# Step 0 of a sparse attention kernel in 105 steps a tile: TensorE's products laid on other steps, with more steps between VectorE and TensorE

## The chip, the cores and the metric

The kernel runs on one core of a Trainium2 chip. The core has five engines that run side by side, each through its own queue of instructions in order: TensorE (PE, matrix products, with a queue of weight loads, PEld), VectorE (DVE), ScalarE (ACT), GpSimd (POOL) and SyncE (SP, which here only issues DMAs). An instruction that needs the result of another engine waits at the head of its queue, and all that stands behind it waits too. The metric is the device time of one execution in microseconds (us), as the median of several runs.

## The reference

Two layers work on 3327 nodes with 256 features. Layer 0 is a graph attention over a sparse 0/1 adjacency with a gated update. Layer 1 makes two steps of a propagation over that adjacency and, beside it, of an attention that keeps for each row only the largest probabilities up to a sum of 0.9:

```python
def _top_p_attention(X, W1, W2, W3):
    q = X @ W1.T @ W2.T
    k = X @ W3.T
    logits = q @ k.T / TAU
    probs = jax.nn.softmax(logits, axis=-1)
    idx = jnp.argsort(-probs, axis=-1)
    sp = jnp.take_along_axis(probs, idx, axis=-1)
    cs = jnp.cumsum(sp, axis=-1)
    keep_sorted = cs - sp < TOP_P
    ...
    A = probs * mask
    return A / jnp.maximum(A.sum(-1, keepdims=True), 1e-12)
...
for n in range(STEPS):                 # STEPS = 2
    A = _top_p_attention(Xa, W1, W2, W3)
    Xf = R @ Xf
    Xa = A @ Xa
    Z = Z + Xf @ U1[n].T + Xa @ U2[n].T
```

Each layer ends with a layer norm over the input plus the layer's result. The change is in the first of the two steps (n = 0, "step 0").

## The kernel before

The 3327 rows are 26 tiles of 128 (the last has 127). Layer 0 runs to about 400 us, step 0 of layer 1 from there to about 1000 us, then step 1, then the layer's end. In step 0 few keys are kept by a whole tile of 128 rows, so the kernel does not multiply by all 3327 keys: it finds the keys that any row of the tile keeps (at most 640), gathers those, and works the attention out on them alone. For one tile (function `sparse`), in this order, with the names that the profile uses:

- pl: logits of the tile against all keys, in four pairs of products of 416 columns (L1542), copied by ACT to SBUF (`array`, L1545). DVE takes the eight largest of each group of 208 (the "eights", L1558) and sorts these candidates into a list of 40 (L1576, L1578); nmax is minus the largest.
- g1, m1, pxf: POOL gathers the neighbours' rows of x (L631), DVE makes a 0/1 matrix (m, L1286), PE multiplies (pxf, L1299 and L1301), ACT scales (xf, L1317), and a DMA writes the rows out. This is R @ Xf. xb (L1715) is a sum that POOL makes for the end of the layer.
- Exp of all logits with their sums (L1306, L1312) and of the list (e, L1314); a running sum and comparisons (L1322 to L1340) give `limit`, for each row minus a threshold between the lowest logit kept and the highest dropped.
- Signs of logits minus limit (ACT L1345, L1347; DVE L1350, is_ge) are summed over the rows by 26 small products (pc, L1355); any (L1362) says which keys some row keeps, two products (pp) number them, and DVE works out from that two one-hot matrices (upto L1370 to high L1382; hot L1387, L1389, L1390, L1392). Their 26 products (pu, L1397) are the list of kept keys. It goes over node (ACT L1402, DVE L1404) through DRAM and back (L1405, L1407).
- POOL turns it into row numbers (uidx, L1410) and gathers the kept keys' rows (g from x1k, five gathers, L1414). PE transposes the keys (pk, L1435 and L1437), ACT copies them (kg), PE makes the logits of the kept keys minus limit (plt, L1448 and L1454; diag holds limit), ACT takes Exp (w, L1460), DVE sets those under the limit to 0 (w, L1462), PE multiplies with the rows (pav, L1466), DVE takes the reciprocal of the sum (rA, L1469), ACT scales (xa, L1473), and `qk` makes query and key of step 1 (ptq, xtq, pq, qT, kT).

`sparse` is a generator. `yield from to(n)` lets n - done phases go by, so that a tile's work is cut into steps. `step_0` (L1480) starts a tile every EVERY0 = 16 phases and in each phase runs every tile that is under way one step further, the oldest first. About six tiles are in work at any time, and what runs together is what has the same step number modulo 16. The order so written is the order of the queues of PE, ACT, DVE and POOL (`manual_schedule`). Waits between engines are put in by the framework, by regions of tiles that overlap. `first_1` fetches the rows for step 1's first tile and, as tiles end, makes its logits; the last pair of these needs all 26 tiles. Tiles of psum and SBUF come from pools with a fixed number of buffers (`bufs`), and taking one waits until the use before last (with two) has been read. The pool `psm` with its tag "sm" has two and serves pc, pp, pu, ptq and pq.

The call of each tile at its phase:

```python
while self.phase < EVERY0 * NT or tiles:
    if self.phase % EVERY0 == 0 and self.phase // EVERY0 < NT:
        tiles.append(self.sparse(self.phase // EVERY0))
    for g in list(tiles):
        if next(g, True):
            tiles.remove(g)
            self.done += 1
```

## Time and profile before

| what | us |
|---|---|
| median of 3 runs | 1859.94 (1857.53 to 1861.38) |
| the profiled execution | 1862.22, its span 1860.4 |
| busy in the span: PE, DVE, POOL, ACT | 1565.4, 1442.2, 1083.6, 1032.6 |
| DVE's first instruction of step 0's list (upto), tile 0 and tile 25 | 418.5 and 952.7 |
| PE busy, 600 to 700 us, at a granted clock of 0.86 | 83.44 of 100 |
| DVE busy, 600 to 700 us | 79.94 of 100 |
| PE busy, 1100 to 1400 us (step 1), clock 1.00 | 290.21 of 300 |

The page counts an engine as busy while an instruction runs; a wait is put down to the instruction that ended last before it. Lines "A <- B: us, times, longest" name the instruction that waited and the one waited for. In the timeline a row has the start, the duration, the engine, the line in the kernel, the operation with output and inputs, the count of equal instructions put together, and in brackets the idle time before it. "Granted clock" is the share of full speed that PE had.

### The profile page before, as it was taken

Reading aid. Unit: us, or ns where it says so; the run is one execution under the profiler, and the core shown is the slowest. Engines: PE = TensorE matmul, PEld = TensorE weight load, DVE = VectorE, ACT = ScalarE, POOL = GpSimd, SP = SyncE. Lnnn points to the kernel's source line nnn. Section 1 sums busy time; section 2 is a strip of 40 time slices with the busy share of each in tenths; the row PEclk is TensorE's granted clock in tenths of the full one; section 3 lists DMA queues with packets and bytes.
Section 4 is the critical chain, followed back from the end, with each engine's and each line's share of the span. In section 5 each row is a group of like instructions: output and inputs, shape, how many; then the busy total and the mean of one; then the engine's idle time right before and its main releaser. Section 6 shows DMA issues by size and latency. Waiting matters only on the chain. (4 is left out here: it accounts for less than half of the span.)

```text
span 1860.4 us, 28927 instructions
## 1 busy us (share of the span) xinstructions
PE 1565.4 (84%) x8425; PEld 1105.7 (59%) x8425; DVE 1442.2 (78%) x4835; ACT 1032.6 (56%) x2388; POOL 1083.6 (58%) x1800
## 2 busy tenths in 40 slices
PE   6489998986788888788876999999999989788992
PEld 5255555644555555555544777777777656677882
DVE  5788887358887888888736999999999877967751
ACT  3366666645655666565633555555555536568554
POOL 2577777535555555555463666556666573756654
PEclk9799999977888888888877999999999989899996
DMA  8877773232333333333331111111111120223321
GB/s 272 298 255 231 232 229 86 69 88 76 90 91 84 85 82 94 91 89 91 93 81 36 46 49 46 46 49 53 53 50 52 47 59 21 69 60 99 98 88 45
DMA packets 113862, 180.07 MB, mean 97 GB/s; under 512 B 27740, under 2 KB 82773, under 8 KB 113696
## 3 DMA queue, kind: packets, MB, share of 16 engines
q0 software_dynamic: 26624, 74.64, 15.2%
q1 hardware_dynamic: 68818, 86.65, 14.4%
q10 hardware_dynamic: 18254, 16.86, 2.8%
q8 instruction: 69, 1.13, 0.3%
q14 instruction: 97, 0.79, 0.1%
HBM read 146.08 MB, written 32.09 MB: 96 GB/s over the span
## 5 line engine op out<-in xcount | busy, mean ns | idle before, releaser
L1759 PE MATMUL pav<-xa,at 128*128 128x256 f32 (+2 forms) x1352 | 329.6, 388 | 7.3 <-ACT at L1745 7.0
L1545 ACT COPY array<-pl 128x416 f32<-128x416 f32 (+3 forms) x402 | 183.2, 508 | 209.2 <-PE pl L1542 201.8
L1759 PEld LDWEIGHTS pav<-xa,at 128*128 128x128 f32 (+2 forms) x1352 | 244.8, 190 | 86.6 <-ACT at L1745 39.2
L1558 DVE MAX8 cand<-array 128x8 f32<-128x167 f32 (+5 forms) x921 | 244.0, 337 | 18.6 <-ACT array L1545 15.0
L1542 PE MATMUL pl<-kT,qT 64*128 64x416 f32 (+3 forms) x804 | 224.2, 588 | 16.9 <-ACT array L1545 11.4
L631 POOL DMA_INDIRECT g<-xf_rows,edge x130 | 136.7, 1052 | 154.8 <-PE pxf L1702 124.2
L1745 ACT COPY at<-pt 128x512 f32<-128x512 f32 (+2 forms) x182 | 96.1, 542 | 138.0 <-PE pt L1743 87.2
L631 POOL DMA_INDIRECT g<-whx,edge x130 | 140.9, 1084 | 46.7 <-issue 36.0
L631 POOL DMA_INDIRECT g<-x_rows,edge x130 | 137.1, 1054 | 50.9 <-issue 43.9
L1414 POOL DMA_INDIRECT g<-x1k,uidx x130 | 140.8, 1083 | 39.0 <-issue 31.7
L1466 PE MATMUL pav<-g,w 128*128 128x257 f32 (+1 forms) x260 | 106.8, 588 | 31.9 <-DVE w L1462 29.5
L1576 DVE MAX8 lst<-cand 128x8 f32<-128x160 f32 (+3 forms) x364 | 114.1, 313 | 8.1
L1542 PEld LDWEIGHTS pl<-kT,qT 64*128 64x128 f32 (+1 forms) x804 | 77.7, 195 | 65.1 <-issue 29.4
L1466 PEld LDWEIGHTS pav<-g,w 128*128 128x128 f32 (+1 forms) x260 | 76.7, 307 | 54.0 <-DVE w L1462 32.1
L848 DVE FIND_INDEX8 at<-ones,array 128x8 uint32<-128x840 f32 (+1 forms) x104 | 105.5, 1027 | 0.0
L1371 POOL COPY needed<-upto 128x1 f32<-128x1 f32 x26 | 4.8, 185 | 158.5 <-DVE upto L1370 158.5
L1674 DVE MATCH_REPLACE8 array<-gone,array 128x3335 f32<-128x3335 f32 (+1 forms) x26 | 94.0, 3617 | 0.0
L1578 DVE MATCH_REPLACE8 cand<-lst,cand 128x160 f32<-128x160 f32 (+3 forms) x312 | 92.9, 298 | 0.0
L1694 POOL TENSOR_SCALAR m<-col,erow 128x128 f32<-128x128 f32 x130 | 76.8, 604 | 1.0
L1301 PE MATMUL pxf<-g,m 128*128 128x256 f32 (+1 forms) x260 | 69.4, 416 | 1.9 <-DMA g<-x_rows,edge 1.2
L969 PE MATMUL acc<-g,m 128*128 128x259 f32 (+1 forms) x260 | 64.9, 397 | 6.8 <-ACT m L965 6.8
L1702 PEld LDWEIGHTS pxf<-g,m 128*128 128x128 f32 (+1 forms) x260 | 49.4, 198 | 34.0 <-issue 24.0
(564 smaller groups left out, 3869.7 us busy)
## 6 DMA issues: line engine op xcount, KB each, us to landing
array<-in_adj_dram SPq DMA_DIRECT2D x23, 1248.0 KB
array<-in_adj_dram SPq DMA_DIRECT2D x23, 415.5 KB
xf_rows<-xf SPq DMA_DIRECT2D x50, 128.0 KB
xa_rows<-xa SPq DMA_DIRECT2D x50, 128.0 KB
xfs<-xf_rows SPq DMA_DIRECT2D x50, 128.0 KB
whx<-table ACTq DMA_DIRECT2D x25, 129.5 KB
x_rows<-x ACTq DMA_DIRECT2D x25, 128.0 KB
x1k<-x ACTq DMA_DIRECT2D x25, 128.0 KB
```

What stands on the lines that cost most here:

```text
L631: self.nc.gpsimd.indirect_dma_start(out=dst[:, b, :], out_offset=None, in_=table[:, :], in_offset=bass.IndirectOffsetOnAxis(ap=self.edge[: ...
L848: nc.vector.max_index(at[:r, g, :], self.ones8[:r], ad[:r, g, :])
L1414: nc.gpsimd.indirect_dma_start(out=g2[:, b, :], out_offset=None, in_=sh.x1k[:, :], in_offset=bass.IndirectOffsetOnAxis(ap=idx[:, b : b + 1 ...
L1466: nc.tensor.matmul(acc[:r, : D + 1], w[:, b, :r], g2[:, b, : D + 1], start=(b == 0), stop=(b == UB - 1))
L1542: nc.tensor.matmul(pl[:r, :w], q[on], self.sh.kT[on, n, s : s + w], start=True, stop=True)
L1545: nc.scalar.copy(l[:r, h * HALF + s : h * HALF + s + w], pl[:r, :w])
L1558: self.nc.vector.max(cand[:r, g * 8 : g * 8 + 8], src[:r, g * group : min(N, (g + 1) * group)])
L1576: nc.vector.max(lst[:r, k : k + 8], cand[:r])
L1578: nc.vector.match_replace(cand[:r], lst[:r, k : k + 8], cand[:r], -BIG)
L1674: nc.vector.match_replace(rev, gone[:r], rev, -BIG)
L1745: nc.scalar.copy(at[:, :full, :r], pt[:, :full, :r])
L1759: nc.tensor.matmul(v.acc[: v.r, :D], at[:k, j - 4 * g, : v.r], V[:k, j, :], start=(j == 0), stop=(j == NT - 1))
```

## The change

The same work is laid on other steps. A tile takes 105 steps in place of 93; EVERY0 stays 16, so that between six and seven tiles are in work at a time. In a table (place = step modulo 16):

| work | engine | step before (place) | step after (place) |
|---|---|---|---|
| m1 | DVE | 15 (15) | 7 (7) |
| pxf, six pairs of products | PE | 18 (2) | 21 and 22 (5, 6) |
| xf and its rows out | ACT, SP | 23 (7) | 25 (9) |
| bound, is_ge | DVE | 29 (13) | 30 (14) |
| pc | PE | 33 (1) | 33 (1) |
| any | DVE | 35 (3) | 36 (4) |
| pp | PE | 36 (4) | 38 (6) |
| upto to high | DVE | 37 (5) | 43 (11) |
| hot, four products | DVE | 38, 39, 39, 43 (6, 7, 7, 11) | 45, 47, 47, 53 (13, 15, 15, 5) |
| pu | PE | 45 (13) | 57 (9) |
| node copy; node sum, list out and back | ACT; DVE, SP | 47; 49 (15; 1) | 59; 61 (11; 13) |
| uidx and five gathers | POOL | 56 to 61 (8 to 13) | 69 to 74 (5 to 10) |
| diag; pk | ACT; PE | 67 (3) | 75; 77 (11; 13) |
| kg; plt; w's Exp | ACT; PE; ACT | 70; 72; 74 (6; 8; 10) | 79; 82; 84 (15; 2; 4) |
| w's mask; pav; rA | DVE; PE; DVE | 78; 80; 83 (14; 0; 3) | 86; 89; 93 (6; 9; 13) |
| xa and its rows out | ACT, SP | 87 (7) | 95 (15) |
| ptq; xtq; pq; qT and kT | PE; ACT; PE; ACT | 89; 89; 91; 91 (9, 11) | 98; 100; 102; 104 (2, 4, 6, 8) |

The copy of the number of kept keys (needed) goes from POOL to DVE. `first_1` starts at phase 431 in place of 430. The logits, eights, sort, Exps and the gathers of g1 keep their steps. The diff:

```diff
--- before.py
+++ after.py
@@ -1280,7 +1280,7 @@
                 sh.gather(g1, sh.x1_rows, t, ((1, 2, 3, 5, 6).index(step),))
             if step == 7:
                 self.x_and_bias(t)
-            if step == 15:
+            if step == 7:
                 m1 = work.tile([P, EB, P], F32, tag="m", name=f"m{tag}")
                 for b in range(EB):
                     nc.vector.tensor_scalar(m1[:, b, :], sh.col1, sh.erow[:, t, b : b + 1], None, ALU.is_equal)
@@ -1295,10 +1295,6 @@
         yield from to(18)
         next(sort)
         next(sort)
-        acc1 = self.pac.tile([P, 512], F32, tag="av", name=f"pxf{tag}")
-        nc.tensor.matmul(acc1[:r, :D], self.ident[:r, :r], sh.x1[:r, t, :], start=True, stop=False)
-        for b in range(EB):
-            nc.tensor.matmul(acc1[:r, :D], m1[:, b, :r], g1[:, b, :], start=False, stop=(b == EB - 1))
         both = self.p[t % 2].bitcast(BF16)
         signs, hot = both[:, : N + 1], both[:, N + 1 : N + 1 + NT * 2 * (UL + UH)].rearrange("p (b e) -> p b e", b=NT)
         sums = small("sums", f"sums{tag}", 2)
@@ -1310,9 +1306,15 @@
         nc.vector.memset(e[:, 0:1], 0.0)
         yield from to(21)
         nc.scalar.activation(signs[:r, HALF:N], l[:r, HALF:N], AF.Exp, bias=nmax[:r], accum_out=sums[:r, 1:2])
+        acc1 = self.pac.tile([P, 512], F32, tag="av", name=f"pxf{tag}")
+        nc.tensor.matmul(acc1[:r, :D], self.ident[:r, :r], sh.x1[:r, t, :], start=True, stop=False)
+        for b in range(2):
+            nc.tensor.matmul(acc1[:r, :D], m1[:, b, :r], g1[:, b, :], start=False, stop=False)
         yield from to(22)
         nc.scalar.activation(e[:r, 1:], lst[:r, : LIST[0] - 1], AF.Exp, bias=nmax[:r])
-        yield from to(23)
+        for b in range(2, EB):
+            nc.tensor.matmul(acc1[:r, :D], m1[:, b, :r], g1[:, b, :], start=False, stop=(b == EB - 1))
+        yield from to(25)
         xf2 = work.tile([P, D], F32, tag="xf2", name=f"xf2_{tag}")
         nc.scalar.activation(xf2[:r], acc1[:r, :D], AF.Copy, scale=sh.rinv[:r, t : t + 1])
         move_rows(nc.sync, sh.xf_rows[t * P : t * P + r, :], xf2[:r], r)
@@ -1345,6 +1347,7 @@
         nc.scalar.activation(signs[:r, s0:s1], l[:r, s0:s1], AF.Sign, bias=limit[:r])
         yield from to(29)
         nc.scalar.activation(signs[:r, s1:s2], l[:r, s1:s2], AF.Sign, bias=limit[:r])
+        yield from to(30)
         bound = small("bound", f"bound{tag}")
         nc.vector.tensor_scalar(bound[:r], limit[:r], -1.0, None, ALU.mult)
         nc.vector.tensor_scalar(signs[:r, s2:N], l[:r, s2:N], bound[:r], None, ALU.is_ge)
@@ -1355,20 +1358,20 @@
             nc.tensor.matmul(
                 pc[:, b : b + 1], signs[:r, b * P : (b + 1) * P], self.ones16[:r, 0:1], start=True, stop=True
             )
-        yield from to(35)
+        yield from to(36)
 
         any_ = small("any", f"any{tag}", NT, BF16)
         full = s2 // P
         nc.vector.tensor_scalar(any_[:, :full], pc[:, :full], 0.5 - r, None, ALU.is_gt)
         nc.vector.tensor_scalar(any_[:, full:], pc[:, full:NT], 0.5, None, ALU.is_gt)
-        yield from to(36)
+        yield from to(38)
         pp = self.psm.tile([P, 512], F32, tag="sm", name=f"pp{tag}")
         nc.tensor.matmul(pp[:, :NT], sh.lower16, any_, start=True, stop=True)
         nc.tensor.matmul(pp[:, NT : 2 * NT], self.ones16, any_, start=True, stop=True)
-        yield from to(37)
+        yield from to(43)
         upto = small("upto", f"upto{tag}", NT)
         nc.vector.tensor_tensor_scan(upto, pp[:, NT : 2 * NT], self.zeros, 0.0, ALU.add, ALU.add)
-        nc.gpsimd.tensor_copy(self.needed[:, t : t + 1], upto[:, NT - 1 :])
+        nc.vector.tensor_copy(self.needed[:, t : t + 1], upto[:, NT - 1 :])
         at = small("at", f"at{tag}", NT)
         nc.vector.tensor_tensor(at, upto, pp[:, NT : 2 * NT], ALU.subtract)
         nc.vector.tensor_tensor(at, at, pp[:, :NT], ALU.add)
@@ -1383,29 +1386,29 @@
         wide = lambda a, n: a.unsqueeze(2).to_broadcast([P, NT, n])
         deep = lambda a, n: a.unsqueeze(1).to_broadcast([P, NT, n])
         e0, e1, e2, e3 = UL, 2 * UL, 2 * UL + UH, 2 * (UL + UH)
-        yield from to(38)
+        yield from to(45)
         nc.vector.tensor_tensor(hot[:, :, e0:e1], wide(low, UL), deep(self.places_l, UL), ALU.is_equal)
-        yield from to(39)
+        yield from to(47)
         nc.vector.tensor_tensor(hot[:, :, e1:e2], wide(high, UH), deep(self.places_h, UH), ALU.is_equal)
         nc.vector.tensor_scalar(hot[:, :, :e0], hot[:, :, e0:e1], self.fromend, None, ALU.mult)
-        yield from to(43)
+        yield from to(53)
         nc.vector.tensor_tensor(hot[:, :, e2:e3], hot[:, :, e1:e2], wide(self.block, UH), ALU.mult)
-        yield from to(45)
+        yield from to(57)
 
         pl = self.psm.tile([P, 512], F32, tag="sm", name=f"pu{tag}")
         for b in range(NT):
             nc.tensor.matmul(
                 pl[:e1, : 2 * UH], hot[:, b, :e1], hot[:, b, e1:e3], start=(b == 0), stop=(b == NT - 1)
             )
-        yield from to(47)
+        yield from to(59)
         node = work.tile([UL, UH], F32, tag="node", name=f"node{tag}")
         nc.scalar.activation(node, pl[UL:e1, UH : 2 * UH], AF.Copy, scale=float(P))
-        yield from to(49)
+        yield from to(61)
         nc.vector.tensor_tensor(node, node, pl[:UL, :UH], ALU.add)
         nc.sync.dma_start(self.ulist[t].rearrange("(l h) -> l h", h=UH), node)
         back = small("back", f"back{tag}", UB)
         nc.sync.dma_start(back, self.ulist[t].rearrange("(p b) -> p b", b=UB))
-        yield from to(56)
+        yield from to(69)
         idx = small("uidx", f"uidx{tag}", UB, U32)
         nc.gpsimd.tensor_scalar(idx, back, -1.0, float(N + 1), ALU.mult, ALU.add)
         g2 = work.tile([P, UB, KX], F32, tag="hx", name=f"g2{tag}")
@@ -1418,15 +1421,18 @@
             )
 
         gather(0)
-        yield from to(57)
+        yield from to(70)
         gather(1)
-        yield from to(58)
+        yield from to(71)
         gather(2)
-        yield from to(59)
+        yield from to(73)
         gather(3)
-        yield from to(61)
+        yield from to(74)
         gather(4)
-        yield from to(67)
+        yield from to(75)
+        diag = work.tile([P, P], F32, tag="xa2", name=f"diag{tag}")
+        nc.scalar.activation(diag[:r, :r], self.ident[:r, :r], AF.Copy, scale=limit[:r])
+        yield from to(77)
 
         pt = self.ptr.tile([P, 512], F32, tag="tr", name=f"pk{tag}")
         for b in range(UB):
@@ -1435,13 +1441,11 @@
                 nc.tensor.matmul(pt[DA:, on], k, self.ident, start=True, stop=True)
             else:
                 nc.tensor.transpose(pt[:DA, on], k, self.ident)
-        diag = work.tile([P, P], F32, tag="xa2", name=f"diag{tag}")
-        nc.scalar.activation(diag[:r, :r], self.ident[:r, :r], AF.Copy, scale=limit[:r])
-        yield from to(70)
+        yield from to(79)
         kg = work.tile([P, (UB + 1) // 2, P], F32, tag="xt", name=f"kg{tag}", bufs=4)
         nc.scalar.copy(kg[:, : UB // 2, :], pt[:, : UB // 2 * P].rearrange("p (j c) -> p j c", c=P))
         nc.scalar.copy(kg[:DA, UB // 2, :], pt[:DA, UB // 2 * P : (UB // 2 + 1) * P])
-        yield from to(72)
+        yield from to(82)
 
         pls = [self.ptr.tile([P, 4, P], F32, tag="tr", name=f"plt{tag}_{k}") for k in range(2)]
         for k, n in enumerate(((UB + 1) // 2, UB // 2)):
@@ -1454,28 +1458,29 @@
             nc.tensor.matmul(
                 pls[b % 2][:, b // 2, :r], kg[on, b // 2, :], self.q(0, t)[on], start=False, stop=(b + 2 >= UB)
             )
-        yield from to(74)
+        yield from to(84)
         w = work.tile([P, UB, P], F32, tag="at", name=f"w{tag}", bufs=3)
         for k, n in enumerate(((UB + 1) // 2, UB // 2)):
             nc.scalar.activation(w[:, k::2, :r], pls[k][:, :n, :r], AF.Exp)
-        yield from to(78)
+        yield from to(86)
         nc.vector.scalar_tensor_tensor(w[:, :, :r], w[:, :, :r], 1.0, w[:, :, :r], ALU.is_ge, ALU.mult)
-        yield from to(80)
+        yield from to(89)
         acc = self.pac.tile([P, 512], F32, tag="av", name=f"pav{tag}")
         for b in range(UB):
             nc.tensor.matmul(acc[:r, : D + 1], w[:, b, :r], g2[:, b, : D + 1], start=(b == 0), stop=(b == UB - 1))
-        yield from to(83)
+        yield from to(93)
         rA = small("rA", f"rA{tag}")
         nc.vector.tensor_scalar(rA[:r], acc[:r, D : D + 1], 1e-30, None, ALU.max)
         nc.vector.reciprocal(rA[:r], rA[:r])
-        yield from to(87)
+        yield from to(95)
         xa = self.xa[:r, t, :]
         nc.scalar.activation(xa, acc[:r, :D], AF.Copy, scale=rA[:r])
         move_rows(nc.sync, sh.xa_rows[t * P : t * P + r, :], xa, r)
-        yield from to(89)
-        for _ in sh.qk(self.psm, self.work, 1, t, xa):
+        yield from to(98)
+        for k, _ in enumerate(sh.qk(self.psm, self.work, 1, t, xa, "sm")):
             yield
-            yield
+            if k < 2:
+                yield
 
     def step_0(self):
 
@@ -1496,7 +1501,7 @@
     def first_1(self):
 
 
-        while self.phase < EVERY0 * NT + 14:
+        while self.phase < EVERY0 * NT + 15:
             yield
         v = self.item(NT)
         self.item(NT + 1)
```

## The prediction

> **What bounds the kernel now.** I read the page's slices first: TensorE (PE) runs at 7 or 8 tenths of its clock for the stretch from about 400 to 1000 us and at full clock before and after. That stretch is step 0, the only code in the diff. Then the table by stage.
>
> ```profile
> 478.30:911.40 433.10, 354.60 (x2382) 232.84 (x2384) 352.51 (x1421) 257.63 (x541) 237.06 (x260) 0.84 0.33 88
> ```
>
> Columns: PE, weight loads, VectorE (DVE), ScalarE (ACT), GpSimd (POOL), granted clock, DMA share, GB/s. The window runs from one start of L1370 to the same line 20 tiles later, so a tile takes 433.1 / 20 = 21.66 us. No engine is full. So next, DVE's waits in it (us in total, times, longest):
>
> ```profile
> DVE upto L1370 <- PE pp L1367: 35.2, 21, 1.7
> DVE any L1362 <- PE pc L1355: 20.6, 18, 1.8
> DVE rA L1469 <- PE pav L1466: 7.0, 11, 0.7
> DVE any L1362 <- PE pxf L1301: 2.4, 1, 2.4
> ```
>
> With 1.0 more in small pieces that is 66.2 us, 3.31 a tile: take it away and DVE's queue alone needs 18.35. All of it is for PE. PE's own waits in the same window:
>
> ```profile
> PE pav L1466 <- DVE w L1462: 26.7, 19, 1.8
> PE pu L1397 <- DVE p L1392: 17.4, 10, 1.7
> PE pu L1397 <- DVE array L1392: 15.5, 9, 1.7
> ```
>
> So the two wait for each other once a tile. The timeline shows the ring: pav starts when DVE has masked w (619.39), runs 4.65, then logits and pc; DVE's any (626.35) and upto (630.4) wait behind them; the 11 us of DVE work after upto lead to the next w.
>
> ```profile
> 616.63 1.00 PE L1397 MATMUL pu<-p 128*64 128x40 bf16 x26 [1.74 <-DVE p L1392]
> 619.39 4.65 PE L1466 MATMUL pav<-g,w 128*128 128x257 f32 x10 [1.77 <-DVE w L1462]
> ...
> 977.43 2.43 PE L1466 MATMUL pav<-g,w 128*128 128x257 f32 x10 [0.82 <-DVE w L1462]
> ```
>
> The same ten products took 2.43 in the drain. Why 4.65 here, the clock by stretch says:
>
> ```profile
> 614.90:618.40 3.50, 1.00 (x26) 0.90 (x26) 3.33 (x13) 2.34 (x3) 2.59 (x4) 1.00 0.50 130
> 618.40:625.30 6.90, 5.91 (x14) 3.70 (x14) 5.50 (x25) 0.93 (x3) 4.09 (x4) 0.51 0.45 108
> ```
>
> A stretch with two gaps is followed by 6.9 us at half clock, into which pav falls, so the wait lengthens what is waited for.
>
> **The change, part by part.** A profiled execution of 1862.22 us (span 1860.4) is what I subtract from; the median, 1859.94, lies 2.3 lower.
>
> *Positions.* A phase runs every live tile one step, so a step's place between tiles is its number modulo 16. I lay DVE's work out on the new places, with start-to-start times of the timeline: 0 eights and last 1.3; 1 to 3 the sort .75, 1.4, .95; 4 any and eights 1.3; 5 hot's last product .64; 6 w's mask .73; 7 m1 .98; 8 eights 1.12; 9 the running sum .93; 10 limit 1.41; 11 upto to high 1.7; 12 eights 1.15; 13 rA, node, first hot 1.4; 14 is_ge .9; 15 two hots 1.88: 18.5. Then each wait:
> - any: between the end of is_ge and any lie places 15 and 0 to 3, 6.3 us of DVE work; PE has one logits group (.9) and pc (.66) ahead. It waits no more. Today pav (4.65) and logits (1.6) stand ahead.
> - upto: 6.9 us of DVE work since any; PE owes pq .55 and pp .13. Today pxf (2.68) and pk (1.29) are ahead of pp.
> - rA: 7.4 us after w's mask; PE owes the rest of pxf 1.3, logits .9 and pav 2.43 at full, 4.02 at half clock: 4.6 to 6.2. No wait.
> - node's addition, .36 later: pu adds .81 to 1.36, ACT's copy about .5: 5.9 to 8.1 against 7.8. At half clock .3 late.
> - PE: w's mask is two places and 2 us ahead of pav, hot's last product 3.5 us ahead of pu; neither waits for DVE.
>
> So 3.31 a tile goes. *Added to DVE:* the copy to needed, about .1 (.18 long, pipelined). *Off POOL:* that copy held POOL's queue 127.1 us in the window, the gathers of g and xb behind it. It goes; POOL is then tied to the index list's return (L1410).
>
> *The collision.* L1390 takes 1.34 or 1.35 in 23 of 26 tiles and .43 to .54 in the three where xb doesn't run beside it:
>
> ```profile
> 611.15 1.35 DVE L1390 TENSOR_SCALAR p<-p,fromend 128x832 bf16<-128x832 bf16 x1
> ...
> 611.51 0.75 POOL L1715 TENSOR_TENSOR xb<-x,ln_b 128x256 f32<-128x256 f32 x1
> ```
>
> Today both hang on upto. Afterwards POOL goes idx (at place 0), five gathers of 1.31 each, then xb, near 7 to 8 us, beside m1; L1390 is at 17. Saved: 0 to .8; m1 could lose up to .74 of it. I take .4, the middle, as no row has m1 beside xb.
>
> *What is late next.* ACT, from nmax to eights at place 8: Exp 1.66, xtq .27, w's Exps .65, Exp 1.77, e .3, first logits copy .51, hand-overs .14: 5.3; DVE has 5.95 to do. .65 to spare. ACT's node now stands before both Signs (1.05, 1.15) and waits for pu; Signs, logits copy, xa and kg queue behind it, with 2.9 us to spare a tile on ACT. PE at full clock: pav 2.43, four logits 3.6, pxf 2.68, plt 1.95, pk 1.29, pu 1.0, pc .66, pq .55, ptq .35, pp .13: 14.64. One 6.83 us stretch at half clock makes that 18.05, just what DVE needs (18.35 + .1 - .4 = 18.05): then both are full and each small lateness shows. New waits: 0 (clock stays up) to 3.4 (two such stretches: 14.64 + 6.83 = 21.5 a tile). New gaps of 0.6 to 1.2 each, spread over the tile, are nearer to one stretch or none: I take .7. A tile then takes 18.75, 2.91 less.
>
> [...] The stretch above, with gaps of 1.74 and 1.77 about 1.00 of small products, was halved, so I stay with the row.
>
> *The other queues.* m1 moves forward eight steps and is read at step 21: its gathers and its buffer (last read by the tile two before) are long free, so only DVE's order changes, counted above. pxf is cut in two groups of 1.4 and 1.3 in front of pq and pp: if any has come late, pxf's second group is late too, and ACT's xf behind it; 6.9 us lie before the next that needs pp, so 0, at most the 1.3 of the group, and not below nothing, since the products are the same. diag goes ahead of pk, .3 on ACT at place 11, where ACT has its 2.9. ptq, xtq, pq and the copies of qT and kT are spread over six steps: nobody in step 0 reads their result, only the last tile's count at the end. Of their psum buffers (two, five uses a tile) pu's is the nearest: the copies end near place 8, pu is at 9, after pav. 0.
> SP issues the rows of xb (place 7), xf (9), the list out and back (13) and the rows of xa (15) in step order. It waits for POOL 212.8 us in the window today, and nothing but rows for later steps stands behind. The list's return takes some 4 us from node's addition (600.40, back issued 602.86, 1.8 more in the drain's rows), so it is there at place 0 or 1. POOL then has five gathers, xb, and two gathers more, some 10 us, and 2.0 until the last has landed: near 13 us, just when PE comes to pk at place 13. pk late by 1 us makes kg and the next plt late, which have 2 to 3 us; so 0, with 1 us a tile as the upper end and nothing below it, as no one waits for pk today in that window.
>
> *Fill.* DVE waits 6.6 us from 400 to 478; gain 0 to 6.6, I take 3.
>
> *Drain.* Once no new tile begins, the last one's chain sets the end: list, gathers, pk, plt, w, pav, xa, q and k, last logits. Today it takes 69 us from tile 25's step 16 (925.03) to the last logits (993.8). Gone from it: 5.29 at L2219, where DVE waits for POOL's needed. New: tile 25's pu (step 57) stands behind tile 23's pav (step 89 in the same phase); before, pu (45) came ahead of it (80). Tile 23's gathers are queued on POOL behind the ten for step 1, which with their masks hold it 18.9 us (939.35 to 958.21). Followed through by the durations of today's drain (gathers 6.7, landing 2, pk to w 5.4, pav 4, pu 1.5, logits and node 5, list 3.4, and then 21 to the end), a block that begins when tile 22's gathers are out, 8 us after that step 16, puts the end at 77; if only the first five go ahead, at 68. Range -5 to +9; I take +5, because today the block went whole ahead of the next thing on POOL (needed and idx).
>
> **Sum.** 21 tiles x 2.91 = 61, + 3 - 5 = 59. 1862.2 - 59 = 1803, and against the median 1859.94 - 59 = 1801.
>
> **The rivals.**
> - *ACT sets the pace.* Should Exp to copies reach DVE 1 us after its .65 is used, each tile takes 1 us more: 21 less gained, 1822. For it: .65 is the smallest margin and ACT has just been put behind node. Against: 257.63 of 433.1 busy.
> - *The clock (slower).* PE at half clock for more of the tile. It decides from 21.66 - 14.64 = 7.0, that is 14 us at half a tile; at 16 us a tile takes 22.6, 20 lost, with 5 in the drain 1885. For it: at 405 to 427, PE's 13.97 busy of 22 had .66. Against: there gaps made up a third; here PE is 80% busy, as pieces.
> - *Nothing moves.* DVE's three waits reappear behind other products: 1860. Against it, the 6 to 7 us that each now has.
> - *More.* No new waits, L1390's .8 whole, the drain 5 shorter: 17.65, 4.0 x 21 + 6.6 + 5 = 96 gained, 1764; half way, 1775.
>
> **How the numbers follow.** Forecast 0.60 (1785 to 1818), ACT 0.18 (to 1842), clock 0.08, nothing 0.04, more 0.10. Leaving out clock and nothing, and half of more, about 0.17: 1780 to 1842. About 0.2% (3.7 us) can be told from no change here. Faster 0.88, same 0.04, slower 0.08.
>
> **What would show it.** Right: starts of L1370 18 to 19.5 apart; the waits at L1362, L1370 and L1469 under 10 us together; DVE above 93% busy in the steady window; pav no longer waiting for w; L1390 near .5; POOL without the wait at L1371. Wrong: a new DVE wait at the eights for a logits copy or at node; pav still 4 us with clock .8 or less; the drain (last limit to first step 1 list) longer than 10 us beyond today's.

## The result and the profile after

The changed kernel takes 1863.84 us (median; 1853.54 to 1870.37) against 1863.94 for the kernel before beside it (1857.36 to 1869.86): a ratio of 1.0002, 95% interval 0.9987 to 1.0017. No difference can be told; 1801 was forecast. The profiled execution took 1867.8 us, its span 1866.0. Set against the span of before by DVE's upto (before L1370, after L1373) and the last rA:

| stretch | before | after | difference | forecast |
|---|---|---|---|---|
| start to tile 3's upto | 478.3 | 482.2 | +3.9 | -3 |
| tile 3 to tile 23 | 433.1 | 428.3 | -4.8 | -58 |
| tile 23 to tile 25 | 41.3 | 34.7 | -6.6 | -3 |
| tile 25's upto to the last rA | 37.9 | 44.5 | +6.6 | +5 |
| the rest, code that did not change | 869.8 | 876.3 | +6.5 | 0 |

So the forecast fails above all in the steady tiles: 21.42 us a tile, not 18.75. The last row is inside what executions of one kernel differ by.

The windows of after, in the columns of the prediction. The first row is 20 tiles, upto to upto; the others are four stretches of tile 10 of the list:

```profile
482.20:910.50 428.30, 362.24 (x2386) 230.31 (x2386) 348.70 (x1441) 256.27 (x540) 220.05 (x237) 0.81 0.33 87
...
651.40:654.80 3.40, 3.39 (x38) 1.91 (x37) 2.67 (x15) 0.00 (x0) 2.60 (x3) 1.00 0.46 122
654.80:659.10 4.30, 0.00 (x0) 0.00 (x0) 2.69 (x6) 2.91 (x5) 0.40 (x1) 0.76 0.17 54
659.10:662.50 3.40, 3.39 (x33) 2.21 (x34) 3.23 (x16) 2.74 (x7) 0.20 (x1) 0.50 0.14 39
662.50:666.00 3.50, 3.50 (x16) 2.24 (x17) 3.02 (x13) 1.25 (x3) 2.53 (x3) 0.50 0.21 53
```

DVE idles (428.30 - 348.70) / 20 = 3.98 us a tile, before 4.03. The idle time is the same, but the waits are others. The waits of after from 400 to 1000 us (total, times, longest):

```profile
DVE w L1466 <- ACT w L1464: 40.9, 20, 10.1
DVE node L1407 <- ACT node L1405: 34.9, 20, 3.4
DVE cand L1563 <- ACT array L1550: 18.9, 13, 5.0
DVE rA L1473 <- PE pav L1470: 8.1, 3, 3.1
...
DVE any L1365 <- PE pc L1358: 2.4, 1, 2.4
...
PE pl L1547 <- ACT array L1550: 73.7, 27, 5.1
...
ACT node L1405 <- PE pk L1443: 59.9, 12, 7.3
...
ACT node L1405 <- remote: 23.8, 4, 7.0
...
POOL uidx L1413 <- DMA back<-ulist: 170.0, 24, 9.9
```

Of the three waits for PE that the change was costed by, those at upto and any are gone in the 20 tiles (the 2.4 us at any lie outside them); rA keeps 6.3 us there, before 8.0. DVE now waits for ACT, PE for ACT, and ACT in front of node. The line names pk as the releaser, but pk is work for another tile. What node reads is pu. The timeline of after at that tile:

```profile
651.48 1.00 PE L1400 MATMUL pu<-array 128*64 128x40 bf16 x26
651.60 1.00 POOL L631 DMA_INDIRECT g<-x_rows,edge  x1 [0.30 <-issue]
...
652.41 0.97 PE L1547 MATMUL pl<-kT,qT 64*128 64x416 f32 x4
...
654.21 1.00 POOL L631 DMA_INDIRECT g<-x_rows,edge  x1 [0.30 <-issue]
...
654.49 0.30 PE L1443 MATMUL pk<-ident,g 128*64 128x128 f32 x1
656.17 0.18 ACT L1405 ACTIVATE node<-pu 32x20 f32<-32x20 f32 x1 [5.74 <-PE pk L1443]
656.25 1.13 ACT L1347 ACTIVATE array<-array,limit 128x1024 bf16<-128x1024 f32 x1
656.38 0.16 DVE L1407 TENSOR_TENSOR node<-node,pu 32x20 f32<-32x20 f32 x1 [2.10 <-ACT node L1405]
...
658.55 0.91 ACT L1550 COPY array<-pl 128x416 f32<-128x416 f32 x2
658.92 0.43 DVE L1393 TENSOR_SCALAR p<-p,fromend 128x832 bf16<-128x832 bf16 x1
...
659.11 2.16 PE L1547 MATMUL pl<-kT,qT 64*128 64x416 f32 x4 [4.32 <-ACT array L1550]
```

pu's last product ends at 652.48. ACT has been idle for 5.74 us and still starts node only at 656.17: 3.69 us in which no engine computes what node needs. While ACT stands there, the finished logits are not copied, so PE runs out of psum for the next ones and idles for 4.3 us; then come 6.9 us at half clock (the windows above). From the first product of pu to node it takes 3.90 us in the median of the tiles.

That delay was in the trace of before, in its timeline and in its waits of ACT:

```profile
639.07 1.58 PE L1397 MATMUL pu<-array 128*64 128x40 bf16 x26 [1.72 <-DVE array L1392]
...
642.22 1.02 POOL L631 DMA_INDIRECT g<-x_rows,edge  x1 [0.30 <-issue]
...
643.22 0.18 ACT L1402 ACTIVATE node<-pu 32x20 f32<-32x20 f32 x1 [1.63 <-remote]
```

```profile
ACT node L1402 <- remote: 25.9, 21, 1.7
```

Products done at 640.65, node at 643.22, ACT idle for the last 1.63 of it and no releaser found ("remote"). The median from pu to node is 4.10 us there, as long as after. But in the old order node stood behind Signs and copies of logits, and DVE's addition two more places on: only 25.9 us in all were seen as a wait, and DVE's ring with PE covered them.

### The profile page after: what moved, and what is told of

Same layout as the page of the kernel before. It is cut to its first block, busy times and chain, and to the rows that moved or that the text cites. A ratio compares the mean times of both kernels' runs of the same rounds, so it can differ in the third digit from the quotient of the medians.

```text
span 1866.0 us, 28806 instructions
## 1 busy us (share of the span) xinstructions
PE 1582.8 (85%) x8425; PEld 1106.1 (59%) x8425; DVE 1438.1 (77%) x4861; ACT 1031.0 (55%) x2388; POOL 1069.4 (57%) x1774
## 5 line engine op out<-in xcount | busy, mean ns | idle before, releaser
L1547 PE MATMUL pl<-kT,qT 64*128 64x416 f32 (+3 forms) x804 | 247.4, 633 | 83.4 <-ACT array L1550 73.7
L1547 PEld LDWEIGHTS pl<-kT,qT 64*128 64x128 f32 (+1 forms) x804 | 87.4, 210 | 128.0 <-ACT array L1550 84.0
L631 POOL DMA_INDIRECT g<-x_rows,edge x130 | 132.5, 1019 | 53.4 <-issue 38.1
L1417 POOL DMA_INDIRECT g<-x1k,uidx x130 | 134.1, 1032 | 44.2 <-issue 29.8
L1413 POOL TENSOR_SCALAR uidx<-back 128x5 uint32<-128x5 f32 x26 | 5.1, 198 | 170.2 <-DMA back<-ulist 170.0
L1405 ACT ACTIVATE node<-pu 32x20 f32<-32x20 f32 x26 | 4.6, 178 | 117.8 <-PE pk L1443 59.9
L1470 PE MATMUL pav<-g,w 128*128 128x257 f32 (+1 forms) x260 | 66.6, 405 | 3.0 <-DVE w L1466 3.0
```

What stands on the lines that cost most here:

```text
L631: self.nc.gpsimd.indirect_dma_start(out=dst[:, b, :], out_offset=None, in_=table[:, :], in_offset=bass.IndirectOffsetOnAxis(ap=self.edge[: ...
L1417: nc.gpsimd.indirect_dma_start(out=g2[:, b, :], out_offset=None, in_=sh.x1k[:, :], in_offset=bass.IndirectOffsetOnAxis(ap=idx[:, b : b + 1 ...
L1547: nc.tensor.matmul(pl[:r, :w], q[on], self.sh.kT[on, n, s : s + w], start=True, stop=True)
```

## The experiments

I call **hold** the time from the end of a group of small products to PE's raising of the count that the reader waits for, which the trace records (some records are missing, and then the reader's start has to tell); a group is held above 0.3 us. In the texts on record: the first series asks whether the hold (A), the new order of ACT and PE (B) or the ring of list and POOL (C) sets the tile.

**Without gathers by row number, on chip 11.** The ten gathers of a tile become SP's plain loads of the first 640 rows, and uidx falls away. The rows are then not those of the list, and step 1 takes its slow way for lack of sparse rows, at 10399 us in all, which the expectation had not foreseen; only step 0 is read.

```diff
-                sh.gather(g1, sh.x1_rows, t, ((1, 2, 3, 5, 6).index(step),))
+                b = (1, 2, 3, 5, 6).index(step)
+                nc.sync.dma_start(g1[:, b, :], sh.x1_rows[b * P : (b + 1) * P, :])
...
-            nc.gpsimd.indirect_dma_start(
...
+            nc.sync.dma_start(g2[:, b, :], sh.x1k[b * P : (b + 1) * P, :])
```

> Step 0 of the changed kernel with no gather on POOL: the ten gathers a tile (five for g1, five for g2) are replaced by ten loads of the first 640 rows on SP, at the same steps, with the same bytes, and the conversion of the list to row numbers is left out, so that the wrong rows are used and nobody waits for the list. It leaves that part of the computation out. Theory A (pu's result is handed to ACT 2 to 6 us after its products because POOL issues gathers beside them, and node, at the head of ACT's queue ahead of both Signs, passes that delay on to PE and DVE): from pu's first product to node falls from a median of 3.8 us to about 1.0, DVE's waits for node (34.9 us) and for w (40.9) mostly go, the tile takes 18 to 19.5 in place of 21.4, the whole 1805 to 1825. Theory B (the order of PE and ACT itself: pl stands behind the copies of logits, node behind xa and kg, whatever POOL does): the tile stays within 0.5 us of 21.4, the whole 1850 to 1865. Theory C (the list's way through DRAM and POOL's ten gathers set the tile): the time falls as in A, but pu to node need not.

A tile takes 17.29 us. The window, then the timeline:

```profile
480.00:840.00 360.00, 328.63 (x2489) 213.24 (x2487) 343.25 (x1499) 260.42 (x562) 0.00 (x0) 0.98 0.34 101
```

```profile
649.89 1.00 PE L1401 MATMUL pu<-array 128*64 128x40 bf16 x26
...
650.92 0.18 ACT L1406 ACTIVATE node<-pu 32x20 f32<-32x20 f32 x1 [2.06 <-PE pu L1401]
```

node starts 0.03 us after the products (1.03 from the first), and so in 23 of 26 tiles; the last pu but one alone has a gather beside it, one of step 1, and it is held for 0.66 us. DVE is busy 95% of the time, the clock is at 0.98. The order itself does what was forecast of it, and more; but this kernel takes away the gathers, POOL's part and the list's wait together.

**Three moves of steps, on chip 11.** node and its sum later (59 to 62, 61 to 63); the gathers of g1 at steps 0 to 4; both.

```diff
-        yield from to(59)
+        yield from to(62)
         node = work.tile([UL, UH], F32, tag="node", name=f"node{tag}")
...
-        yield from to(61)
+        yield from to(63)
         nc.vector.tensor_tensor(node, node, pl[:UL, :UH], ALU.add)
```

```diff
-            if step in (1, 2, 3, 5, 6):
-                sh.gather(g1, sh.x1_rows, t, ((1, 2, 3, 5, 6).index(step),))
-            if step == 7:
+            if step < EB:
+                sh.gather(g1, sh.x1_rows, t, (step,))
+            if step == 4:
```

> The changed kernel with node's copy on ACT at step 62 in place of 59 (place 14, behind both Signs at 12 and 13) and its addition on DVE at 63 in place of 61 (place 15); POOL's gathers and everything else stay. Theory A: pu's hand-over is as late as before (3 to 5 us from its first product), but Signs and the copies of logits no longer stand behind it; ACT's wait at node falls from about 106 us in the stretch 400 to 1000 to under 40, the tile takes 18.5 to 20, the whole 1805 to 1840. Theory B: no more than 0.5 us a tile, 1852 to 1865. Theory C: the list goes out 2 to 3 us later in the tile, so uidx, the gathers and pk come later, and the time is the same or up to 40 us longer.

> The changed kernel with the five gathers of g1 at steps 0 to 4 in place of 1, 2, 3, 5, 6, and xb at 4 in place of 7, so that on POOL all of these stand ahead of uidx and only g2's five behind it. Nothing else is moved. Theory A: what is beside pu is now g2's gathers alone; the train behind uidx is 3.4 us shorter (two gathers of 1.31 and xb of 0.75), so pu's hand-over comes up to 3 us earlier, where the train ends before it; the tile 19 to 21, the whole 1815 to 1855. Theory B: unchanged, 1855 to 1865. Theory C: the ring pu, list, uidx, gathers, pu is 3.4 us shorter, the tile about 18.5, the whole 1805 to 1815.

> The changed kernel with both of the last two edits: node behind the Signs (steps 62 and 63) and g1's gathers and xb ahead of uidx. Theory A: as node late alone, or up to 10 us better, 1800 to 1835. Theory B: 1852 to 1865. Theory C: as the gathers alone or worse by the later list, 1805 to 1850.

Measured: 1857.12 us, ratio 0.9942 (0.9923 to 0.9961); 1883.06, 1.0071 (1.0047 to 1.0096); 1869.24, 1.0008 (0.9992 to 1.0024). A tile takes 20.63, 22.09 and 21.19. Theory A's times were met in none of the three; the first lies in B's range, the others in nobody's. With node late the hold stays (median 3.49 us) and only less stands behind it: 0.6% of the time. The gathers moved forward lie beside pu still, in 24 of 26 tiles, and all 24 are held. So these three could not part the theories.

**Which part of the missing gathers, on chip 9.** The gathers as plain loads that POOL issues at the same places, behind the same wait for the list; and the kernel before with SP's loads.

```diff
-                sh.gather(g1, sh.x1_rows, t, ((1, 2, 3, 5, 6).index(step),))
+                b = (1, 2, 3, 5, 6).index(step)
+                nc.gpsimd.dma_start(g1[:, b, :], sh.x1_rows[b * P : (b + 1) * P, :])
...
-            nc.gpsimd.indirect_dma_start(
...
+            nc.gpsimd.dma_start(g2[:, b, :], sh.x1k[b * P : (b + 1) * P, :])
```

> Step 0 of the changed kernel with the ten gathers a tile issued by POOL, at the same places of its queue and still behind the wait for the list, but as plain loads of the first 640 rows in place of gathers by row numbers. The wrong rows are used, so that part of the computation is left out, and as step 1 then takes its slow exact way, only the stretch up to step 0's end is read. Theory A (it is the gathers by row number, on POOL beside PE's groups, that delay PE's hand-over): pu's first product to node is 1.0 us in nearly every tile, and the tile is 17.3 to 18.5 us, as without any work on POOL (17.29), though POOL still waits for the list. Theory C (the list's way through DRAM into POOL's queue, ahead of g and pk, sets the tile): the tile is above 19.5, with waits for the list, g and pk like those of the changed kernel.

> The kernel before with the same ten loads of the first 640 rows on SP in place of POOL's gathers, and without the conversion of the list; the same parts are left out and only step 0 is read. If the order of before was bound by the ring between DVE and PE that the prediction named (pav, then any and upto), its tile stays at 20.5 to 21.7 us with DVE's waits for pc and pp of 50 us and more in twenty tiles, and the change is then worth the difference to 17.29, about 4 us a tile, which the gathers took back. If the gathers bound before as well, its tile falls to 17.5 to 19 and the new order was never worth more than about 1 us.

In both the rows loaded are the first 640 and only step 0 is read. The tile of the first takes 17.36 us with pu to node in 1.04, though POOL waits 221.4 us for the list. So neither the list's wait sets the tile nor the order of ACT and PE (B). What the gathers themselves take on POOL is missing here; the next two kernels have it, and answer the rest of C. The tile of before without gathers takes 20.49, with nothing held, and its waits of DVE from 400 to 1000 us are those of the prediction's ring:

```profile
DVE upto L1371 <- PE pp L1368: 44.7, 25, 3.3
DVE any L1363 <- PE pc L1356: 24.3, 23, 1.3
DVE rA L1464 <- PE pav L1461: 14.2, 5, 5.5
```

On the same chip the order is therefore worth some 20.49 - 17.36 = 3.13 us a tile (forecast: 2.91); the second kernel also leaves out the list's wait, which the first keeps.

**Two that seemed to cure it, on chip 9.** With the gathers in place: pu's 26 products made twice; and node at step 63, its sum at 65, all from uidx on two steps later.

```diff
-        for b in range(NT):
+        for b in list(range(NT)) * 2:
             nc.tensor.matmul(
```

```diff
-        yield from to(59)
+        yield from to(63)
...
-        yield from to(61)
+        yield from to(65)
...
-        yield from to(69)
+        yield from to(71)
```

> The changed kernel with pu's 26 products made twice into the same place, the second time over the first. If what holds the hand-over is a price for each small product while POOL gathers, pu's first product to node grows from 4.0 to 6 us or more (another 1.0 for the products and another 2 to 3 for the hold), and the whole by 30 to 60 us. If the hand-over is only held until POOL's train of gathers ends, it stays at 4 to 5 us, and the whole grows by 0 to 20 us.

> The changed kernel with node's copy at step 63 and its addition at 65 (behind Signs, xa and kg), uidx and the gathers two steps later (71 to 76), and all from diag to the queries and keys two steps later (pk at 79, pav at 91, qk at 100), so that pav comes behind pu. Theory A: the hold is as long (pu to node 5 to 7 us), but pk, plt and w have 2.3 us more for it: DVE's wait for w (39.0 with node late alone) goes under 20, pk's wait for g (32.5) under 12, the tile 19 to 20.2 us, the whole 1815 to 1845. Theory B: no gain over node late alone, 1850 to 1865. Theory C: no gain over node late alone, since the ring through list and POOL is as long.

1781.74 us (one run, 1862.28 before on that chip) and 1793.36, ratio 0.9628 (0.9605 to 0.965). Neither was expected: the first was to grow, the second to take 1815 us at the least. Twice the products, and a tile takes 17.80 us. Its timeline:

```profile
647.63 1.82 PE L1400 MATMUL pu<-array 128*64 128x40 bf16 x52
...
648.30 1.00 POOL L631 DMA_INDIRECT g<-x_rows,edge  x1 [0.31 <-issue]
...
649.49 0.18 ACT L1405 ACTIVATE node<-pu 32x20 f32<-32x20 f32 x1 [2.87 <-PE pu L1400]
```

A gather runs beside pu in 25 tiles, and in all of them node starts within 0.04 us of the products. DVE is busy 344.58 of 360 us (480 to 840) at a clock of 0.98 and waits for nothing from tile 3 to tile 23, which is what the forecast was for. Two readings were left: something in these programs (pav is not directly ahead of pu, H1; the count of products, H2), or something outside them.

**The program, on chip 10.** pav moved behind pu; the kernel before with pu made twice; 26 more products behind pu into columns that nobody reads; and the later steps with pu twice.

```diff
-        yield from to(89)
+        yield from to(91)
         acc = self.pac.tile([P, 512], F32, tag="av", name=f"pav{tag}")
...
-        yield from to(93)
+        yield from to(95)
```

```diff
+        for b in range(NT):
+            nc.tensor.matmul(
+                pl[:e1, 256 : 256 + 2 * UH], hot[:, b, :e1], hot[:, b, e1:e3], start=(b == 0), stop=(b == NT - 1)
+            )
         yield from to(59)
```

> The changed kernel with pav two steps later (91, place 11, in place of 89), and with it rA (95), xa (97) and the queries and keys (100); everything up to w's mask stays. pu then stands behind logits and ahead of pav, as in the version with all of it later, in which the hold was gone in 24 of 26 tiles. H1 (the hold needs pu to follow pav directly): the hold is gone, pu to node about 1.0 us, the tile 17.8 to 19, the whole 1785 to 1815. H2 (the hold hangs on how many small products the group has: 26 were held, 52 not): the hold stays at 2 to 4 us in most tiles, the whole 1845 to 1870, and the version with all of it later was quick for its longer slack alone.

> The kernel before with pu's 26 products made twice. In before, pu follows a wait for DVE and not pav. H2 (number of products): the hold of 1.8 to 3.1 us in 23 of 26 tiles goes, and the tile falls from 21.66 towards the 20.49 that it has without gathers, less than 1 us of the doubled group of products showing; the whole 1835 to 1860. H1 (pav directly ahead): the hold was never pav's there, so doubling changes nothing but adds up to 1.0 us a tile: 1862 to 1885.

> The changed kernel with 26 more products of the same kind and size directly behind pu's 26, into columns of the same psum tile that nobody reads; node waits for the first 26 alone. If the hold ends only when enough small products come behind pu (the second 26 pushed the first out), pu's first product to node is 1.0 to 2 us and the tile near 17.8, the whole 1780 to 1795. If it is the length of the group that is handed over that counts, node still comes 3 to 5 us after pu's first product, and the whole is 1850 to 1885.

> The version with all of it later (1793.4, tile 18.16) with pu's products made twice as well. If the hold was the only thing that the doubling took away, there is next to none left to take here, and the second 26 products cost up to 0.9 us of PE a tile: 1793 to 1815. If the doubling helps by keeping PE's clock up, as PE is then busier, the tile falls to 17.6 to 17.9 and the whole to 1778 to 1790.

1859.36 us, ratio 0.9953 (0.9914 to 0.9991); 1878.41, 1.0064 (1.0042 to 1.0087); 1874.23 (one run); 1913.51, 1.0234 (1.0199 to 1.0269), outside both of its forecasts. pu's count is late in all of them. With pav behind, 9 of 15 tiles with a gather beside pu are held and none of 11 without; pc has the gathers beside it now, and 22 of 23 are held. In the kernel before with pu twice it is 25 of 25, in the later steps with pu twice 23 of 25. With the 26 more products only 1 of 12 is held behind its last product, but 11 of the 12 groups beside a gather take more than 2 us for their 52 products, where those without take 1.82. (node did not wait for the first 26 alone: the trace has one count for the 52, at their end. So this kernel has not tested whether later products push a count out.) Neither what stands ahead of pu nor the count of products undoes it. In the last kernel the waits show PE itself stopping among the 52 products, with no releaser:

```profile
PE pu L1400 <- issue: 72.1, 102, 1.2
```

**The chip, on chip 15.** No new edit: the changed kernel, the two of chip 9 once more, and the kernel before.

> The changed kernel as it is, beside the next two on one chip. Theory P (the hold belongs to the program: the order of the queues makes it): the hold is there as in the first profile, 2 to 5 us in 20 tiles and more, the whole 1855 to 1870, whatever the chip does to the others. Theory K (the hold belongs to the chip: the two quick versions ran on one chip, chip 9, and all profiles with the hold on others): on a chip with the hold 1855 to 1870; on a chip without it the hold is under 0.1 us in most tiles, the tile 17.3 to 18.5 and the whole 1780 to 1810.

> The version with all of it later again (1793.4 us and hold in 2 of 26 tiles on chip 9). Theory P: 1788 to 1800 on any chip, hold in few tiles. Theory K: on a chip with the hold, 2 to 5 us of hold in most tiles and 1830 to 1870; on one without, 1788 to 1800.

> The changed kernel with pu's products made twice again (1781.7 us and no hold on chip 9). Theory P: 1778 to 1790 on any chip. Theory K: on a chip with the hold, 4 us and more of hold in most tiles, as in the kernel before with the products twice (4.8), and 1870 to 1920; on one without, 1778 to 1790.

> The kernel before as it is, for its profile on the same chip. Theory P: hold of 1.8 to 3.1 us in 23 of 26 tiles, tile 21.66. Theory K: on a chip with the hold the same; on one without, pu's result is handed over at once, and the time is the same within 8 us (1855 to 1870), since node has slack there and its tile is set by the ring of DVE and PE: without any gather it is still 20.5.

| program | on chip 9 | on chip 15 |
|---|---|---|
| changed kernel | not run | 1864.96, ratio 1.0004 (0.9987 to 1.0021), tile 21.41 |
| node and list later | 1793.36, 0.9628 (0.9605 to 0.965), tile 18.16 | 1875.12, 1.0072 (1.0046 to 1.0099), tile 21.91 |
| pu twice | 1781.74 (one run), tile 17.80 | 1869.92, 1.0027 (1.001 to 1.0043), tile 21.81 |
| kernel before | 1862.28 | 1863.87 (1863.74 in the profiled run) |

The window of the later steps, on chip 9 and then on chip 15:

```profile
480.00:840.00 360.00, 323.55 (x2367) 212.78 (x2368) 343.86 (x1430) 255.45 (x536) 238.12 (x240) 0.89 0.40 105
```

```profile
480.00:840.00 360.00, 301.94 (x1950) 191.19 (x1949) 287.67 (x1178) 214.24 (x442) 194.10 (x196) 0.81 0.32 86
```

One program with a gather beside 25 of its groups of pu: on one chip none is shown to be held (in one the record is missing, and the next, of pav, comes at 2.38 us as in the tiles around it), on the other all 25, by 7.07 us in the median. There DVE waits for the next count in PE's order, that of pav, behind pu's:

```profile
DVE rA L1473 <- remote: 46.0, 13, 4.2
```

With pu twice on chip 15, 4 of 15 groups of pu beside a gather are held behind the last product and 13 of the 15 take more than 2 us, as none of the 11 without does; 14 of 16 of pc are held, and PE stops inside pu for 24.4 us in all. So the program alone (P) does not make the hold: it goes with the chip, or with the time at which that chip was used (K), since each was seen in one series only. The kernel before takes the same time on both; its ring of DVE and PE, I take it, covers the hold. It was not profiled on chip 9.

**A kernel that keeps the gathers away, on chip 3.** POOL copies one column of node ahead of g1's gathers, which move to steps 11 to 15, so that they wait until pu has been handed over; uidx goes to 67, pav to 90, and node's sum to 60 in a buffer of its own. The second kernel is the same without POOL's copy and that buffer.

```diff
-            if step in (1, 2, 3, 5, 6):
-                sh.gather(g1, sh.x1_rows, t, ((1, 2, 3, 5, 6).index(step),))
+            if step > 10:
+                sh.gather(g1, sh.x1_rows, t, (step - 11,))
...
+        nc.gpsimd.tensor_copy(small("held", f"held{tag}")[:UL], node[:, 0:1])
+        yield from to(60)
```

> The changed kernel with POOL kept quiet while pu runs: a copy of one column of node on POOL, behind ACT's copy, stands ahead of g1's five gathers (now at steps 11 to 15, with xb), so that these start when pu has been handed over and run while the list is on its way; uidx and g2's five are at 67 to 71, in front of the next pu; pav is one step later (90) and so behind pu, node's addition one earlier (60), into a buffer of its own. If the hold is what small products suffer while POOL gathers beside them (on chips that have it): pu to node 1.0 to 1.5 us in most tiles, the tile 17.8 to 19.5 and the whole 1785 to 1825 on any chip. If the hold comes whether or not a gather runs at that moment: 3 us and more as before, 1850 to 1890 on a chip with it.

> The same without the copy on POOL and the buffer of its own for the sum: the same order of the gathers, but nothing keeps g1's from starting right behind g2's, beside pu. If the copy's wait is what works: on a chip with the hold it is back, 2 to 5 us in most tiles, the tile 20.5 to 22 and the whole 1845 to 1880; on a chip without it 1785 to 1815. If the new order alone works: as the version with the copy.

1850.58 us, ratio 0.9882 (0.9844 to 0.9919), and 1894.47, 1.0148 (1.01 to 1.0195): POOL's copy and the buffer are worth 1.0148 - 0.9882 = 2.7% of the time before, and by its ratio the first is the fastest on any chip with the hold; by which way is not shown. It missed its 1785 to 1825 and did not keep the gathers away: still 23 of 24 groups of pu beside a gather are held (median 4.46): the list came late, and now the gathers of g2 lie there, as the timeline shows:

```profile
643.41 1.00 PE L1400 MATMUL pu<-array 128*64 128x40 bf16 x26
...
643.86 1.00 POOL L1419 DMA_INDIRECT g<-x1k,uidx  x1 [0.30 <-issue]
...
647.78 1.00 POOL L1419 DMA_INDIRECT g<-x1k,uidx  x1 [0.30 <-issue]
...
649.81 0.18 ACT L1405 ACTIVATE node<-pu 32x20 f32<-32x20 f32 x1 [5.04 <-PE pk L1445]
```

POOL's five gathers follow each other without a gap of more than 0.3 us, and node comes 1.03 us after the last one ends (648.78).

**All runs together.** Groups of 26 small products (pu and pc) in step 0, by whether a gather by row number runs beside them:

| kernel | chip | gather beside: groups, held | none beside: groups, held |
|---|---|---|---|
| before, twice profiled | not named, 15 | 56, 52 | 48, 0 |
| after, twice profiled | not named, 15 | 55, 52 | 49, 0 |
| node late; g1 first; both | 11 | 84, 81 | 72, 0 |
| pav behind | 10 | 38, 31 | 14, 0 |
| node and list later | 15 | 28, 28 | 24, 0 |
| POOL's copy, with and without | 3 | 74, 71 | 30, 0 |
| no gathers by row number | 11 | 2, 2 | 50, 0 |
| sum of these | | 337, 317 | 287, 0 |
| pu twice; later; two without gathers | 9 | 78, 0 | 130, 0 |

Outside chip 9 the hold follows the gathers. The kernels with 52 products there are not in the table; in the two of them whose groups lie partly beside gathers (the 26 more, chip 10, and pu twice, chip 15), 24 of 27 groups of pu beside one take more than 2 us and none of 25 without. A few records are missing, so that single groups could be counted otherwise. Two of the three kernels without them ran on chip 9, where gathers hold nothing either, so they witness against B and C but not for A; that rests on the kernel on chip 11, on the last two columns, and on the one program that took 1793 us without the hold and 1875 with it.

## Why the prediction was wrong

**The step that failed** is in what is late next: "pu adds .81 to 1.36, ACT's copy about .5: 5.9 to 8.1 against 7.8." The sum prices products and copy and sets the hand-over between them at nothing. From pu's first product to node, the two terms up to node's start, it gave 0.81 to 1.36; the median in the result is 3.90. The second half followed from it: "ACT's node now stands before both Signs ... and waits for pu; Signs, logits copy, xa and kg queue behind it, with 2.9 us to spare a tile on ACT." The queue was named and its spare time too, and the delay used more than it. Behind node stand these waits (400 to 1000 us): PE for ACT's copies (73.7 us), DVE for w (40.9), for node (34.9) and for the eights' logits (18.9), POOL for the list (170.0). The one reading of the old trace that would have told it, the timeline from pu to node, was not made; it shows 2.57 us at the tile above.

**DVE's three waits** (3.31 us a tile): right where nothing is held. With pu twice on chip 9 DVE waits for nothing in the 20 tiles. In the changed kernel any and upto wait for nothing there and rA for 6.3 us; where the hold is longest (later steps, chip 15) rA's wait is back, with 77 us from 400 to 1000. In the sum for rA the 4.02 for pav stands in no row; with the 4.65 shown it is 6.9 against 7.4, still no wait. DVE's own queue, put at 18.05, was nearly right: the changed kernel's window less its waits gives (428.3 - 64.0) / 20 = 18.22, and pu twice on chip 9 a tile of 17.80 without any wait.

**The collision**, "I take .4": L1393 (L1390 before) takes 0.42 to 0.53 in all tiles, 0.92 less in 23 of 26. But xb now runs beside m1 in 12 of 26 tiles, and there the five instructions of m1 take 1.52 to 2.12 in place of 1.06:

```profile
667.87 2.12 DVE L1286 TENSOR_SCALAR m<-col,erow 128x128 f32<-128x128 f32 x5
...
669.16 0.73 POOL L1720 TENSOR_TENSOR xb<-x,ln_b 128x256 f32<-128x256 f32 x1
```

In the mean of the 20 tiles 0.88 is saved and 0.38 lost: 0.50, near the .4 and by the trade that the prediction had named.

**PE and its clock**, one half-clock stretch and 0.7 of new waits: the stretch is in the trace of before, 6.83 us at 0.50 (618.47 to 625.30), behind one with the two gaps that itself had 1.00. The granted clock of 0.81 is near what one such stretch a tile would give, but by another way, behind a gap that the hold made: the 4.30 us without a product above came before 6.9 at 0.50. Three of the kernels without hold have 0.97 to 0.98 (480 to 840 us) and no new waits. But in the later steps on chip 9 nothing is held either, PE's longest wait from tile 3 to tile 23 is 2.1 us, and the clock is still 0.89. Two stretches of that kernel, with a wait of 1.90 us across their border:

```profile
661.31:664.72 3.41, 2.40 (x34) 1.32 (x33) 3.34 (x10) 2.16 (x8) 2.98 (x2) 1.00 0.34 99
664.72:668.13 3.41, 2.52 (x6) 1.50 (x6) 3.17 (x17) 2.04 (x4) 1.00 (x1) 0.50 0.48 88
```

So the prediction's row was no exception: here too a stretch in which PE was idle for a part of the time, busy 2.40 of 3.41 us, came before one at 0.50. What sets the clock, no run was made to find.

**The list and POOL.** "The list's return takes some 4 us": from node's sum to uidx it was 5.6 to 6.0 us in most tiles of the changed kernel, 3.1 to 5.0 in most on chip 9, and the sum itself was late; POOL idled 170.0 us. "pk near 13 us, just when PE comes to pk", priced at 0, held: PE's wait for pk's rows came to 0.3 us in the 20 tiles. With pu twice on chip 9 POOL waited 91.3 us for the list and DVE for nothing, so the list cost nothing there.

**Fill and drain.** The drain became 6.6 us longer (+5 taken, -5 to +9 given). The fill lost 3.9 in place of gaining 3.

**The rivals.** "Nothing moves" named the time that came, 1860, and a chance of 0.04, but not the way: DVE's waits did not come back behind other products of PE. ACT did set the pace, yet not by the margin of 0.65 us in front of the eights that this rival was priced by. The clock was 0.81, with a half-clock stretch behind a gap that the hold made, as at the tile above.

**What stays open.** Where the hold arises, no run shows. Two things were measured beside it: in the changed kernel counts held back come out together, 34 to 43 ns apart; and PE stops among 52 products, 102 times for 72.1 us in all with the later steps and pu twice (chip 10), 34 times for 24.4 with pu twice (chip 15), for 1.2 us at the longest in both. That the count waits for the end of a train of gathers fits only in part: in the changed kernel it came 0.2 to 1.1 us behind a train's last gather in 20 of 26 held groups, but in the kernel before the next gather was already running in 23 of 26. This says nothing of chip 9. Nor is it shown whether the row numbers matter or that POOL issues the loads, since the kernel with POOL's plain loads ran on chip 9 alone. The changed kernel was not run on chip 9. That it would have met the forecast there is likely from its two relatives (1781.74 and 1793.36) and is not measured.

## What to carry to other kernels

Before a change takes away the slack behind a result, read in the old trace how long the reader starts after the producer has ended: an idle time with no releaser ("remote") while all inputs are done was here a cost that slack had been hiding (25.9 us seen as a wait, 4.10 us from pu to node in the median tile). Price the hand-over as a term of its own, and ask first what stands behind the reader on its queue. A version that wins on one chip must be run on another before its cause is believed: here 1793 and 1875 us were the same program.

## What the runs showed of the hardware

- A group of 26 small products of TensorE was reported to its reader late while GpSimd ran gathers by row number, in 317 of 337 groups outside chip 9, by 2.36 us (the changed kernel) to 7.07 (node and list later) in the median of pu; without gathers, on chip 11, the reader started 0.03 us after the products. On chip 9 the program with the 7.07 showed it in none of its 25 groups of pu beside a gather.
- Gathers of 1.00 us lay 0.30 apart. In the changed kernel the count came 0.2 to 1.1 us behind the last of a train in 20 of 26 held groups; in the kernel before the next gather was running in 23 of 26.
- With 52 products beside gathers PE itself stopped among them (24.4 us in all with pu twice on chip 15, none on chip 9: 52 products in 1.82 us beside a gather).
- In the changed kernel 4.30 us of idle PE behind such a late report were followed by 6.9 at a granted clock of 0.50. In the later steps on chip 9 0.50 came after a stretch of 3.41 us in which PE was busy 2.40 and no wait was above 2.1.
- Beside the addition of xb on POOL a DVE instruction took 1.34 or 1.35 in 23 of 26 tiles, and 0.43 to 0.54 in the three without it. Moved apart, it took 0.42 to 0.53, and m1's five took 1.52 to 2.12 in place of 1.06 in the 12 tiles where xb ran beside them.
